# Running the last group's chains beside the next graph convolution's first four fifths

## The chip, the cores and the metric

The kernel runs on one core of one Trainium2 chip. The metric is device time in microseconds of one execution. Before the change three runs took 2504.49, 2504.52 and 2510.24 us; their median is 2504.52 us. A core has several engines that work beside each other, each through its own queue of instructions in order: TensorE (PE in the profile; PEld is its weight load), VectorE (DVE), ScalarE (ACT), GpSimd (POOL), and SyncE (SP), which here only issues transfers. They are tied to each other by semaphores.

## The reference

3125 nodes have 256 features each; 100,000 edges connect them. Four blocks follow each other, each of the form x = x + f(layernorm(x)):

1. a two-layer graph attention (four heads, then one);
2. a mixture of experts in which one choice holds for all tokens: the mean row picks two of eight experts, and every node goes through both;
3. a linear layer and two graph convolutions;
4. a routed mixture of experts, two of eight for each node.

The change lies where block 2 hands over to block 3, and where the two convolutions of block 3 meet. What is computed there:

```python
# block 2, after the choice of two experts with weights w_dense
h = gelu(xf @ W1[e] + b1[e]);  y = h @ W2[e] + b2[e]
out = layer_norm(sum_e w_dense[e] * y[e] + xf, gamma, beta)
# block 3
x = relu(input @ weight + bias)
for i in range(2):
    h = x @ conv_w[i]
    x = relu(segment_sum(h[src] * dinv[src] * dinv[dst], dst) + conv_b[i])
```

The segment sum over edges is a product with the matrix of edge counts, which an earlier stage has left in HBM as float16.

## The kernel before, in words

Nodes are padded to 25 blocks of 128 rows (`NB`, `P`); five blocks make a group (`GB`), and there are five groups (`GR`). `self.x` (`x_rows` in the profile) holds all rows. The program is written in an order of its own, but a framework that allots tiles also orders each engine's instructions by its own estimate of when each could start; so the order in which the queues are filled can differ from that of the source. Tiles come from stacked pools: a tile that takes the place of an earlier one has to wait until the earlier one's last readers are done. Where a tile lies thus decides what its first writer waits for.

**Second attention layer** (`graph_attention_fast`, `attend_all`). For each group and each of 25 source blocks DVE makes an exponent's argument `z` (L837), ACT the exponential (L839), DVE the weights `w` by a product with the counts (L845), and PE multiplies them with the rows (L854). There are two tiles for `z` and two for `w`. When a group ends, small tasks for it are taken from a queue `spare`, two at each step: sums to `x_rows` (L1009), then the tasks of `SharedExperts.tasks`: statistics (L1211, L1212), the root (L1216), normed rows into `xa` (L1220), transposes into `xa_t` (L1226, L1227) and their sum (L1231).

**Shared experts** (`SharedExperts.run`). `choose` computes the mean, the routing weights and the two experts' numbers with many small DVE operations on 8 columns (L1253 to L1286), loads the two experts' weights through SP (L1292, L1295), scales the second ones (L1316) and sums the second biases (L1329). POOL then adds the summed bias to `xa` (L1349) and `beta` to `x_rows` (L1350), 25 blocks each; ACT issues the loads of `gamma` and `beta` (L1342, L1344). After that, 256 rows at a time, PE makes the hidden product (L1377), ACT the Gelu (L1380), PE the second product (L1387), DVE the sum (L1390). Between these, `go_on` takes tasks from a queue of this function: for each group that is complete `finish(g)` (norm, L1024 to L1030, times gamma, L1367, added to `x_rows`, L1368), and the tasks that `before(g, tmp)` of the convolutions returns, here called a group's chain: `norm`, five transposes with copies (L1037, L1131), four blocks of the linear layer (L1137, L1140), and for each of five blocks `linear` (L1070), which projects the rows with the convolution's weights, scales them (L1073), cuts them in two parts whose sum is the number (L1075) and writes both to `parts[0]` (L1077 on ACT, L1078 on DVE). When the last block is done, all tasks that are left run, the last group's chain among them, and the room is given back.

**Convolutions** (`graph_convolutions_fast`, `layer`). For each group of five target blocks, five times: SP loads a block of counts (`cnt_h`, three tiles, L1090), ACT converts three fifths of it to the matmul's type (L1093) and DVE two fifths (L1094) into `cnt_r` (two tiles), and PE multiplies, five target blocks by five source blocks, 25 matmuls (L1099). During the first four of the five steps tasks of the queue `spare` are spread over the matmuls. After the fifth step `finish0` or `finish1` is called for each target block: DVE turns the sums into rows `o` (`total`, L1112, L1114), and in the first convolution two tasks are put in the queue, `turn` (transposes, L1037, Relu, L1161) and `linear(1, b, ...)`, the second convolution's projection. After the first convolution's last group a loop `while spare` runs what is left; then `router.open` allots its tiles and issues small loads (L2429 to L2454), and the second convolution starts. Its `finish1` adds to `x_rows` (L1173) and queues the router's tasks.

Of the kernel before, what the change touches and what calls it, by code (L numbers as in the profile page):

```python
# [11 lines left out]
F32 = mybir.dt.float32  # L12
F32R = mybir.dt.float32r
# [748 lines left out]
class Fast(Kernel):  # L762
# [277 lines left out]
    def graph_convolutions_fast(self, I, router, experts, out):  # L1040
# [5 lines left out]
        with ExitStack() as ctx:  # L1046
# [34 lines left out]
            spare = router.spare  # L1081

            def layer(i, work, finish):
                n = GB
                for b0 in range(0, NB, n):
                    pos = {}
                    for j0 in range(0, NB, 5):
                        ch = work.tile([P, 5, GW], F16, name="cnt_h", bufs=3)
                        o = b0 % GB * P
                        nc.sync.dma_start(ch[:, :, :n * P],  # L1090
                                          self.cnt[b0 // GB, :, j0:j0 + 5, o:o + n * P])
                        c = work.tile([P, 5, GW], F32R, name="cnt_r", bufs=2)
                        nc.scalar.copy(c[:, :3, :n * P], ch[:, :3, :n * P])  # L1093
                        nc.vector.tensor_copy(c[:, 3:, :n * P], ch[:, 3:, :n * P])  # L1094
                        for b in range(n):
                            if j0 == 0:
                                pos[b] = psum.tile([P, 512], F32, name="po")
                            for j in range(j0, j0 + 5):
                                nc.tensor.matmul(pos[b], lhsT=c[:, j - j0, ts(b, P)],  # L1099
                                                 rhs=parts[i][:, j].rearrange("p a m -> p (a m)"),  # L1100
                                                 start=(j == 0), stop=(j == NB - 1))
                            if j0 == NB - 5:
                                finish(b0 + b, pos[b])
                                continue
                            left = (NB - 5 - j0) // 5 * n - b
                            for _ in range(-(-len(spare) // left)):
                                spare.popleft()()

            def total(i, b, po, work):
                d = dinv[:, b:b + 1]  # L1110
                o = work.tile([P, D], F32, name="o", bufs=7)
                nc.vector.scalar_tensor_tensor(o, po[:, :D], d, conv_b[:, i, :], op0=ALU.mult,  # L1112
                                               op1=ALU.add)
                nc.vector.scalar_tensor_tensor(o, po[:, D:], d, o, op0=ALU.mult, op1=ALU.add)  # L1114
                return o

            with tc.tile_pool(name="gcn_first", bufs=1, reuse_waits="tile") as first:
                parts[0] = first.tile([P, NB, 2, D], F32R, name="parts0")

                def before(g, tmp):  # L1120
# [21 lines left out]
                    return ([norm] + [lambda b=b: turn(b) for b in range(GB)] +  # L1142
# [4 lines left out]
                with tc.tile_pool(name="gcn_in", bufs=1, reuse_waits="tile") as tmp:  # L1147
                    experts.run(lambda g: before(g, tmp))
                second = ctx.enter_context(ExitStack())
                room = second.enter_context(tc.tile_pool(name="gcn_second", bufs=1, side="right", reuse_waits="tile"))  # L1150
                parts[1] = room.tile([P, NB, 2, D], F32R, name="parts1")
                psum = second.enter_context(tc.tile_pool(name="gcn_po", bufs=5, space=PSUM, reuse_waits="tile"))
                with tc.tile_pool(name="gcn_work0", bufs=1, reuse_waits="tile") as work:
                    def finish0(b, po):
                        o = total(0, b, po, work)
                        turned = []

                        def turn():
                            x_t = work.tile([P, 2, P], F32, name="x_t", bufs=3)
                            turned.append(x_t)  # L1160
                            nc.scalar.activation(x_t, self.turn_block(aux, o), AF.Relu)  # L1161
                        spare.append(turn)
                        spare.append(lambda: linear(1, b, turned[0]))
                    layer(0, work, finish0)
                    while spare:
                        spare.popleft()()
# [4 lines left out]
            def finish1(b, po):  # L1171
                o = total(1, b, po, work)
# [11 lines left out]
class SharedExperts:  # L1184
# [8 lines left out]
    def open(self):  # L1193
        self.rooms = ExitStack()
        pool = self.rooms.enter_context(self.tc.tile_pool(name="ffn0", bufs=1, side="right", reuse_waits="tile"))

        self.xa = pool.tile([P, NB, D], F32, name="xa")
# [133 lines left out]
    def run(self, onward):  # L1331
# [3 lines left out]
        with ExitStack() as ctx:  # L1335
            pool = ctx.enter_context(tc.tile_pool(name="ffn0_w", bufs=1, reuse_waits="tile"))
# [4 lines left out]
            gamma = pool.tile([P, D], F32, name="gamma")  # L1341
            nc.scalar.dma_start(gamma, bcast(I["L0_ffn_gamma"], D))  # L1342
# [19 lines left out]
            def finish(g):  # L1362
                xa = self.xa[:, g * GB:(g + 1) * GB, :]
                k.norm_group(xa, xa, GB, work)
# [5 lines left out]
            for c0 in range(0, NP, n):  # L1370
# [13 lines left out]
                for b in range(c0 // P, c1 // P):  # L1384
# [5 lines left out]
                    nc.vector.tensor_add(self.xa[:, b, :], self.xa[:, b, :], py)  # L1390
                    if b % GB == GB - 1:
# [3 lines left out]
                    go_on(1)  # L1395
            while spare:
                spare.popleft()()
        self.rooms.close()
# [1492 lines left out]
```

## Time and profile before

| What | Value |
|---|---|
| median of three timed runs | 2504.52 us |
| profiled execution, own time | 2363.22 us |
| profiled execution, span | 2361.4 us |
| mean granted PE clock | 0.943 |
| PE, PEld, DVE, ACT, POOL busy | 2052.3, 1712.3, 1335.9, 1084.5, 807.8 us |
| second attention layer | about 1010 to 1294 us of the span |
| choice of experts, until the first expert matmul | 1294 to 1326 us |
| shared experts, with the chains | 1326 to 1567 us |
| first convolution | 1572 to 1739 us |
| second convolution | 1752 to 1935 us |
| routed experts | to the end, 2361 us |

The span is the time from the first to the last instruction of one execution that was taken with the profiler. That execution took 2363.22 us, 141 us less than the median of the timed runs, so its durations give the shape of the work, and sums made from them are compared with it first. A row of the timeline gives the start, the length, the engine, the line, the output and inputs, and in brackets how long the engine had been idle before and what ended that; rows that run into each other are merged, with their number behind an x. "SPq" and "ACTq" are those engines' queues as they issue transfers.

### The profile page before, as it was taken

The page shows a single profiled execution, that of the slowest core. Times are in us where ns is not written, and L with a number is a line of the kernel's source. Part 1 is how long each engine was busy: PE and PEld are TensorE (multiplying, and loading weights), DVE is VectorE, ACT ScalarE, POOL GpSimd, SP SyncE. Part 2 cuts the span into 40 slices and gives each one's busy share as a digit, 9 for nine tenths or more (in the row PEclk, how much of TensorE's full clock was granted, in tenths as well). Part 3 has the DMA queues.
Part 4 walks back from the last instruction along what each step waited for, and adds up shares of the span by engine and source line. Part 5 has one row for each costly group of instructions (what it writes and reads, how often), then busy time and mean ns, then how long its engine had stood idle before and what let it go on. Part 6 is the DMA issues. An engine that isn't in the chain of part 4 may idle for free. (4 is left out here: it accounts for less than half of the span.)

```text
span 2361.4 us, 35957 instructions
## 1 busy us (share of the span) xinstructions
PE 2052.3 (87%) x10512; PEld 1712.3 (73%) x10512; DVE 1335.9 (57%) x4399; ACT 1084.5 (46%) x2496; POOL 807.8 (34%) x801
## 2 busy tenths in 40 slices
PE   5577888878988876999999699979989978999996
PEld 5456677666766655778888588858877767888886
DVE  7898576767777763178888443333326664212221
ACT  3497556555666536044454254434434433222231
POOL 1777777777777723000000500000001223222221
PEclk9899899999999888989999799989999988999998
DMA  7545574756677758962221100023325445667773
GB/s 234 159 122 152 140 209 135 210 165 190 201 196 210 204 154 314 323 220 70 80 74 41 45 1 1 1 99 125 126 99 170 144 136 187 190 189 229 214 214 73
DMA packets 236521, 356.91 MB, mean 151 GB/s; under 512 B 37356, under 2 KB 177923, under 8 KB 232603
## 3 DMA queue, kind: packets, MB, share of 16 engines
q1 hardware_dynamic: 194315, 258.97, 33.8%
q0 software_dynamic: 39008, 92.91, 15.2%
q10 hardware_dynamic: 2992, 2.62, 0.4%
q8 instruction: 88, 1.44, 0.2%
q14 instruction: 118, 0.97, 0.1%
HBM read 268.69 MB, written 86.20 MB: 150 GB/s over the span
## 5 line engine op out<-in xcount | busy, mean ns | idle before, releaser
L1876 POOL DMA_INDIRECT edge_rows<-table,pick x566 | 590.8, 1044 | 183.5 <-issue 78.3
L1961 PE MATMUL edge_sums<-edge_moves,edge_rows 128*128 128x120 f32 x2264 | 332.3, 294 | 76.4 <-DVE agg L1974 75.9
L1961 PEld LDWEIGHTS edge_sums<-edge_moves,edge_rows 128*128 128x128 f32 x2264 | 308.5, 206 | 114.9 <-DVE agg L1974 93.4
L1099 PE MATMUL po<-parts,cnt_r 128*128 128x512 f32 x1250 | 310.1, 403 | 14.0 <-ACT cnt_r L1093 9.3
L1099 PEld LDWEIGHTS po<-parts,cnt_r 128*128 128x128 f32 x1250 | 236.1, 192 | 63.5 <-ACT cnt_r L1093 10.1
L854 PE MATMUL po<-h,w 128*128 128x257 f32 x1250 | 277.2, 383 | 3.5 <-ACT o L1006 2.3
L854 PEld LDWEIGHTS po<-h,w 128*128 128x128 f32 x1250 | 237.8, 192 | 38.5 <-ACT o L1006 3.9
L1764 PE MATMUL ps<-hot_key,hot_lo 128*128 128x350 f16 (+2 forms) x782 | 192.4, 335 | 67.4 <-DVE acc L1790 29.6
L1782 ACT CAST acc<-ps 128x325 f32 (+2 forms) x391 | 178.7, 457 | 134.4 <-PE ps L1764 98.6
L1744 DVE TENSOR_SCALAR hot_key<-iota_key,key 128x350 f16<-128x350 f16 (+2 forms) x782 | 235.9, 329 | 4.2 <-PE ps L1764 3.4
L2759 ACT ACTIVATE hid<-ph,ffn_b 128x256 f32<-128x256 f32 (+1 forms) x232 | 105.6, 455 | 263.1 <-PE ph L2757 260.6
L2757 PE MATMUL ph<-xe,ffn_w 128*128 128x256 f32 (+1 forms) x928 | 194.1, 367 | 3.3 <-DMA ffn_w<-in_L_ffn_W 3.3
L2772 POOL DMA_INDIRECT out<-y,to x53 | 82.6, 1558 | 315.9 <-DVE y L2771 173.3
L2767 PE MATMUL py<-ffn_w,hid 128*128 128x256 f32 x848 | 189.9, 381 | 0.9 <-ACT hid L2759 0.9
L2757 PEld LDWEIGHTS ph<-xe,ffn_w 128*128 128x128 f32 x928 | 165.2, 194 | 26.2 <-DVE rt_xt L1030 3.7
L2767 PEld LDWEIGHTS py<-ffn_w,hid 128*128 128x128 f32 x848 | 159.6, 191 | 21.3 <-ACT hid L2759 1.3
L839 ACT ACTIVATE z<-z,att_cols 128x640 f32<-128x640 f32 x125 | 103.0, 828 | 146.4 <-DVE z L837 120.1
L1750 ACT ACTIVATE hot_lo<-iota_key,lo 128x128 f16<-128x128 f16 x494 | 170.0, 395 | 0.0
L1764 PEld LDWEIGHTS <-hot_lo 128*128 128x128 f16 x782 | 72.8, 104 | 113.2 <-ACT hot_lo L1757 43.1
L1093 ACT CAST cnt_r<-cnt_h 128x1920 fp32r<-128x1920 f16 x50 | 89.9, 1799 | 110.8 <-PE po L1099 101.7
L2433 POOL IOTA earlier<- 128x128 f32 x1 | 0.2, 242 | 395.0 <-PE po L1099 395.0
L845 DVE TENSOR_TENSOR w<-z,cnt 128x640 f32<-128x640 f32 x125 | 102.4, 820 | 41.4 <-PE po L854 38.5
(422 smaller groups left out, 3249.5 us busy)
## 6 DMA issues: line engine op xcount, KB each, us to landing
ffn_w<-in_L_ffn_W SPq DMA_DIRECT2D x58, 1024.0 KB
cnt_h<-cnt SPq DMA_DIRECT2D x50, 800.0 KB
rows<-blank SPq DMA_DIRECT2D x109, 258.0 KB
cnt<-acc SPq DMA_DIRECT2D x50, 400.0 KB
cnt<-cnt SPq DMA_DIRECT2D x25, 800.0 KB
normed<-first_out SPq DMA_DIRECT2D x20, 640.0 KB
first_out<-first SPq DMA_DIRECT2D x56, 192.0 KB
edge_rows<-table,pick POOLq DMA_INDIRECT x566
```

Source lines behind the costliest of these rows:

```text
L839: nc.scalar.activation(z, z, AF.Exp, bias=cols[:, 0, j:j + 1], scale=-1.0)
L854: nc.tensor.matmul(pos[i][:, :D + 1], lhsT=w[:, ts(i, P)], rhs=moving[:, j, :D + 1], start=(j == 0), stop=(j == NB - 1))
L1099: nc.tensor.matmul(pos[b], lhsT=c[:, j - j0, ts(b, P)], rhs=parts[i][:, j].rearrange("p a m -> p (a m)"), start=(j == 0), stop=(j == NB - 1))
L1744: nc.vector.tensor_scalar(h[:, u, :NB * w], self.wide[:, :NB * w], self.key[:, t:t + 1], None, op0=ALU.is_equal)
L1750: nc.scalar.activation(l[:, u, :], self.wide[:, :P], AF.Abs, bias=self.lo[:, t:t + 1], scale=-1.0)
L1764: last = self.nc.tensor.matmul(ps[:, :n], lhsT=l[:, u, :], rhs=h[:, u, :n], start=(u == 0), stop=(u == CT - 1))
L1782: ins = self.nc.scalar.copy(self.acc[g][:, :, ds(o + 1, width(c) - 1)], self.parts[c][:, :, 1:])
L1876: return self.nc.gpsimd.indirect_dma_start(out=self.ring[:, e % (RB * BT), :], out_offset=None, in_=self.table, in_offset=bass.IndirectOff ...
L1961: nc.tensor.matmul(ps[:, f * 4 * w:f * 4 * w + EW], lhsT=self.rows_of(m)[:, e, ts(f, P)], rhs=self.spread[m % 3][:, e * 5 * w:e * 5 * w + EW],
L2757: nc.tensor.matmul(ph, lhsT=w1[:, c, ts(f, P)], rhs=xe[:, c, :], start=(c == 0), stop=(c == 1))
L2759: nc.scalar.activation(hid[:, f, :], ph, AF.Gelu, bias=b1[:, f:f + 1])
L2767: nc.tensor.matmul(py, lhsT=hid[:, f, ts(i, P)], rhs=w2[:, f, :], start=(f == 0), stop=(f == NF - 1))
```

## The change

`SharedExperts.run` no longer runs the last group's tasks itself. At the last block it first runs what the queue still holds (the chain of the group before), then appends `finish` and the chain of the last group, and returns the queue; `graph_convolutions_fast` adds it to `spare`, so `layer` hands it out. Four empty tasks stand in that chain as pauses. To let tiles live long enough, `gamma` and the norm's small tiles come from the pool `gcn_in` (`keep`), which stays open together with `gcn_first` and `gcn_work0` until the first convolution is over; `xa` keeps its room until the first `finish0`, which closes it and takes the room of `parts[1]`; `xa_t` is given back at the end of `run`. The loop `while spare` after the first convolution is gone, so its last group's tasks go to the second convolution; for that `o` and `x_t` come from an outer pool, `gcn_sums`. The tiles for `cnt_h` are two instead of three.

```diff
+            sums = ctx.enter_context(tc.tile_pool(name="gcn_sums", bufs=1, reuse_waits="tile"))
...
-                        ch = work.tile([P, 5, GW], F16, name="cnt_h", bufs=3)
+                        ch = work.tile([P, 5, GW], F16, name="cnt_h", bufs=2)
...
-            def total(i, b, po, work):
+            def total(i, b, po):
                 d = dinv[:, b:b + 1]
-                o = work.tile([P, D], F32, name="o", bufs=7)
+                o = sums.tile([P, D], F32, name="o", bufs=7)
...
-            with tc.tile_pool(name="gcn_first", bufs=1, reuse_waits="tile") as first:
+            room_of = lambda stack, name: stack.enter_context(
+                tc.tile_pool(name=name, bufs=1, reuse_waits="tile"))
+            with ExitStack() as first_rooms:
+                first = room_of(first_rooms, "gcn_first")
                 parts[0] = first.tile([P, NB, 2, D], F32R, name="parts0")
...
-                    return ([norm] + [lambda b=b: turn(b) for b in range(GB)] +
+                    wait = [lambda: None] * 2 if g == GR - 1 else []
+                    return (wait + [norm] + wait + [lambda b=b: turn(b) for b in range(GB)] +
...
-                with tc.tile_pool(name="gcn_in", bufs=1, reuse_waits="tile") as tmp:
-                    experts.run(lambda g: before(g, tmp))
+                tmp = room_of(first_rooms, "gcn_in")
+                spare.extend(experts.run(lambda g: before(g, tmp), tmp))
                 second = ctx.enter_context(ExitStack())
-                room = second.enter_context(tc.tile_pool(name="gcn_second", bufs=1, side="right", reuse_waits="tile"))
-                parts[1] = room.tile([P, NB, 2, D], F32R, name="parts1")
...
+                def finish0(b, po):
+                    if parts[1] is None:
+                        experts.rooms.close()
+                        parts[1] = second.enter_context(tc.tile_pool(
+                            name="gcn_second", bufs=1, side="right", reuse_waits="tile")).tile(
+                                [P, NB, 2, D], F32R, name="parts1")
+                    o = total(0, b, po)
...
-                    layer(0, work, finish0)
-                    while spare:
-                        spare.popleft()()
+                layer(0, room_of(first_rooms, "gcn_work0"), finish0)
...
-    def run(self, onward):
+    def run(self, onward, keep):
...
+            gamma = keep.tile([P, D], F32, name="gamma")
+            nc.scalar.dma_start(gamma, bcast(I["L0_ffn_gamma"], D))
             pool = ctx.enter_context(tc.tile_pool(name="ffn0_w", bufs=1, reuse_waits="tile"))
...
-            gamma = pool.tile([P, D], F32, name="gamma")
-            nc.scalar.dma_start(gamma, bcast(I["L0_ffn_gamma"], D))
             beta = pool.tile([P, D], F32, name="beta")
...
-                k.norm_group(xa, xa, GB, work)
+                k.norm_group(xa, xa, GB, keep)
...
+                    if b == NB - 1:
+                        go_on(len(spare))
                     if b % GB == GB - 1:
                         g = b // GB
                         spare.append(lambda g=g: finish(g))
                         spare.extend(onward(g))
-                    go_on(1)
-            while spare:
-                spare.popleft()()
-        self.rooms.close()
+                    if b < NB - 1:
+                        go_on(1)
+        self.turned.close()
+        return spare
```

More of the change, by code (lines that the diff above doesn't have):

```diff
@@ L1145, in before, with turn @@
                              for b in range(GB)])
-                with tc.tile_pool(name="gcn_in", bufs=1, reuse_waits="tile") as tmp:
-                    experts.run(lambda g: before(g, tmp))
+                tmp = room_of(first_rooms, "gcn_in")
+                spare.extend(experts.run(lambda g: before(g, tmp), tmp))
                 second = ctx.enter_context(ExitStack())
-                room = second.enter_context(tc.tile_pool(name="gcn_second", bufs=1, side="right", reuse_waits="tile"))
-                parts[1] = room.tile([P, NB, 2, D], F32R, name="parts1")
                 psum = second.enter_context(tc.tile_pool(name="gcn_po", bufs=5, space=PSUM, reuse_waits="tile"))
[L1153 to L1163, printed above, removed]
-                    layer(0, work, finish0)
-                    while spare:
-                        spare.popleft()()
+                def finish0(b, po):
[5 more added lines that the diff above has]
+                    o = total(0, b, po)
+                    turned = []
+                    def turn():
+                        x_t = sums.tile([P, 2, P], F32, name="x_t", bufs=3)
+                        turned.append(x_t)
+                        nc.scalar.activation(x_t, self.turn_block(aux, o), AF.Relu)
+                    spare.append(turn)
+                    spare.append(lambda: linear(1, b, turned[0]))
+                layer(0, room_of(first_rooms, "gcn_work0"), finish0)
             router.open(ctx, aux, I)
@@ L1171, in finish1 @@
             def finish1(b, po):
-                o = total(1, b, po, work)
+                o = total(1, b, po)
                 nc.vector.scalar_tensor_tensor(self.x[:, b, :], o, 0.0, self.x[:, b, :],
@@ L1193, in open @@
     def open(self):
-        self.rooms = ExitStack()
-        pool = self.rooms.enter_context(self.tc.tile_pool(name="ffn0", bufs=1, side="right", reuse_waits="tile"))
-        self.xa = pool.tile([P, NB, D], F32, name="xa")
+        self.rooms, self.turned = ExitStack(), ExitStack()
+        room = lambda stack, name: stack.enter_context(
+            self.tc.tile_pool(name=name, bufs=1, side="right", reuse_waits="tile"))
+        self.xa = room(self.rooms, "ffn0").tile([P, NB, D], F32, name="xa")
+        pool = room(self.turned, "ffn0_turned")
         self.xa_t = pool.tile([P, 2, NP], F32, name="xa_t")
```

## The prediction

> **What bounds the kernel now.** I read the page first. TensorE is busy for 2052.3 of 2361.4 us (87%), so time is won where it idles or runs at a lower clock. The table of stages finds these places (columns: stretch, its length, busy time of PE, PE's weight load, DVE, ACT and POOL, granted PE clock, DMA share, GB/s):
>
> ```profile
> core 0: us, PE busy (x) PEld busy (x) DVE busy (x) ACT busy (x) POOL busy (x), PEclk, DMA share, GB/s
> 1294.00:1326.00 32.00, 6.21 (x22) 3.64 (x21) 24.02 (x86) 7.37 (x17) 17.20 (x26) 0.58 0.28 86
> 1544.00:1572.00 28.00, 13.66 (x47) 9.20 (x47) 13.14 (x42) 11.08 (x24) 0.00 (x0) 0.70 0.19 69
> 1572.00:1603.00 31.00, 31.00 (x129) 25.52 (x130) 8.69 (x15) 9.64 (x6) 0.00 (x0) 0.94 0.50 176
> 1738.00:1752.00 14.00, 7.85 (x36) 5.38 (x34) 7.61 (x25) 7.63 (x17) 1.55 (x8) 1.00 0.49 180
> ```
>
> Three thin stages: the choice of experts (1294), the end of the shared experts (1544, the change's first place) and the seam between the convolutions (1738, its second). Next the timeline of the first seam (start, length, engine, line):
>
> ```profile
> 1543.16 0.40 ACT L1077 CAST parts<-split 128x256 fp32r<-128x256 f32 x1 [0.20 <-DVE split L1075]
> ...
> 1565.85 123.32 SPq L1090 DMA_DIRECT2D cnt_h<-cnt  x22
> 1570.12 3.70 ACT L1093 CAST cnt_r<-cnt_h 128x1920 fp32r<-128x1920 f16 x2 [3.02 <-DMA cnt_h<-cnt]
> 1571.97 31.45 PE L1099 MATMUL po<-parts,cnt_r 128*128 128x512 f32 x130 [6.20 <-ACT cnt_r L1093]
> 1579.69 1.80 ACT L1093 CAST cnt_r<-cnt_h 128x1920 fp32r<-128x1920 f16 x1 [5.86 <-PE po L1099]
> 1585.36 1.80 ACT L1093 CAST cnt_r<-cnt_h 128x1920 fp32r<-128x1920 f16 x1 [3.86 <-PE po L1099]
> ```
>
> The first count block is loaded only at 1565.85, lands 4.2 us later, is converted in 1.8 us, and the convolution starts at 1571.97. Conversions follow PE's release: 5.67 us for 25 matmuls, but 7.72 for the first 25, at a granted clock of 0.77. A cold start costs 2.05 us. Then the choice:
>
> ```profile
> 1304.89 17.05 POOL L1350 TENSOR_TENSOR x_rows<-x_rows,beta 128x256 f32<-128x256 f32 x25 [10.55 <-DMA beta<-in_L_ffn_beta]
> ...
> 1307.04 0.65 DVE L1264 TENSOR_SCALAR load<-rw 128x8 f32<-128x8 f32 x1
> ...
> 1319.85 1.21 SPq L1292 DMA_DIRECT2D ffn_w<-in_L_ffn_W  x2
> ```
>
> While POOL adds beta, DVE's little operations with two SBUF inputs or a tensor_scalar take 0.65 us; reciprocals, and the same forms where POOL rests, some 0.2. They lead to the expert numbers, these to the weight loads at 1319.85.
>
> **The change, part by part.** The order in which each engine's instructions are queued in the two built kernels decides what really moves.
>
> *First seam.* In the built order the five projections (L1070) of the group before last still precede the convolution on PE; the last group's chain stands between the 37th and the 100th of the first 125 count matmuls. The loads no longer wait for the chain's tiles: the first waits for PE's last reads of the expert weights (hidden product ended by 1534.6, second product 1538.9), so it lands by 1543.2. On ACT the first conversion stands behind the cast of 1543.16: 1543.56 + 1.80 = 1545.4, where PE can start. The group then is 125 x 0.2267 = 28.3 us, plus the chain's own PE work: 5 pairs of transposes at 0.27 (1.3), 4 weight blocks at 1.07 (4.3), 5 projections at 0.86 (4.3), 9.9 in all. In later groups, five pairs of transposes and projections already run between count matmuls: 34.2 us a group, 28.3 + 5.65 + 0.2 of stall, so such interleaving works. 1545.4 + 28.3 + 9.9 = 1583.6, against 1602.36 before: 18.8 less. I take off 1.3 for stalls: normed rows reach PE about 0.2 late (the first rows' conversion delays DVE by 0.83), ACT's conversions stand ahead of copies of transposes. **-17.5**, between -12 (half the chain's 14 steps wait 0.8 for ACT) and -19.
>
> Does the cover hold? DVE has 8.69 us busy and ACT 9.64 in the 31 us of that group before; the chain is most of the 13.14 and 11.08 of the 28 us ahead, and all of it has 38 us to fit into. Without cover the chain would again cost its 21 us (1545.4 to 1566.7) and the gain be the earlier load and conversion alone.
>
> *Second seam.* Here the built order does not do what the diff says: on PE all five transposes and projections of the last group still stand ahead of the second convolution's first count matmul. Only ACT's and DVE's first conversions move, ahead of the last block's split:
>
> ```profile
> 1747.80 0.41 ACT L1077 CAST parts<-split 128x256 fp32r<-128x256 f32 x1
> ...
> 1750.14 3.48 ACT L1093 CAST cnt_r<-cnt_h 128x1920 fp32r<-128x1920 f16 x2
> 1751.98 36.16 PE L1099 MATMUL po<-parts,cnt_r 128*128 128x512 f32 x151 [3.08 <-ACT cnt_r L1093]
> ```
>
> The block is loaded from 1741.27, so landed by 1745.5; converted from 1748.2 it is ready at 1750.0: -1.9. The pause of PE shrinks from 2.9 us (projections end 1749.1) to 1.0. The Trainium skill ("TensorE: Matmul & The Clock Gate", Part 1) puts half clock after about 3.4 us idle in a free-running window. The row disagrees in size: here 2.9 us were enough to lose it (7.68 us for the first 25 matmuls, clock 0.78). By the rule as written neither seam would start cold; by the row 1.0 us lies far under, and the 1.6 us of the first seam less clearly. I take warm starts: -2.0 more here, **-3.9** in all; between 0 and -4. (The first seam's warm start is in its sum; cold, it is 2.05 worse.)
>
> *Beta.* Gamma moves to the tiles that live on, and with it beta's place. This is no line of the change's plan: in the built order ACT issues beta's load before the second attention layer, not near its end, and POOL puts 20 of the 25 adds ahead of the iota that waits for that layer's end. They run group by group as the rows are normed (L1220). In the choice, 17 DVE operations take 11.2 us from start to start; free ones of 8 columns take 0.20 to 0.27: 17 x 0.22 = 3.7. Gain 7.4, less 0.4 for the last five adds beside the last norms: **-7.0** (-5 to -8.2), all on the path: the numbers release the weight loads, these L1316 and the first Gelu.
>
> *What the 20 adds cost where they go.* PE bounds attention (231.7 of 234 us), two weight tiles deep:
>
> ```profile
> 1081.24 1.38 DVE L1220 TENSOR_SCALAR xa<-x_rows,ln_mv,ln_rstd 128x256 f32<-128x256 f32 x4
> 1082.54 0.81 DVE L845 TENSOR_TENSOR w<-z,cnt 128x640 f32<-128x640 f32 x1
> 1084.39 0.81 DVE L845 TENSOR_TENSOR w<-z,cnt 128x640 f32<-128x640 f32 x1
> ```
>
> PE starts on the first of these tiles at 1083.71, the next at 1086.16: slack 0.4 and 1.0. The Trainium skill ("SBUF — State Buffer", Who interferes with whom) says that GpSimd and VectorE share a port pair, an exclusive lock for the whole instruction. That speaks against the change: by it each add blocks DVE for its 0.72, 20 x 0.72 = 14.4. The rows charge less: L904 runs every 0.87 us beside POOL's bias adds, 0.43 alone, and the choice's operations 0.67 instead of 0.22; 0.44 an add, 8.8 in all. Laying 0.44 an add from 1081.7 on, the first tile comes 0.5 late, the next 0.3 more: 0.8 a group, four groups, **+3.2** (0 to +9, or +14.4 less slack of 4 by the rule).
>
> *The rest.* The conversion buffers before the count tiles go from three to two. A load goes out when a conversion ends and is needed two steps later: 2 x 5.67 - 1.80 = 9.5 us against 4.2 to land; hidden by 5.3. In the second convolution SP's five stores of rows (5.5 us) pass one load, which is then needed some 4 us after landing. Zero. The sums and the turned tile live in an outer pool and the second convolution's parts take their place later: no instruction more. Zero.
>
> Sum: +3.2 - 7.0 - 17.5 - 3.9 = **-25.2**, from 2363.2 of the profiled execution (span 2361.4) to 2338.0. The timed runs have a median of 2504.5, 141 us more; no row says where. Idle time and few PE instructions are concerned, so I carry the difference over unscaled: 2479.3.
>
> **Rivals.** (1) *Attention pays in full.* The lock as in the rule: +10.4 instead of +3.2, 2486.5. For it: two tiles only. Against: the measured 0.44.
> (2) *The chain is not hidden.* PE, in order, waits for ACT behind the conversions at most of the 14 steps; the first seam gives only load, conversion and clock, 4.2 + 1.8 + 2.0 = 8: 2488.8. For it: one in-order ACT queue. Against: the later groups' 0.2 of stall.
> (3) *Slower: two buffers for counts.* If loads took over 9.5 us from issue to landing, each of some 48 steps would wait for the excess at L1093. At 9.5 + 0.53 the whole 25.2 is gone; at 10.3 it is 2504.5 + 13 = 2517. Against: 4.2 measured with two in the queue, and a DMA share of 0.45.
> (4) *No change.* Freed time returns as a later wait. Against: PE is over 90% busy in most later slices, so work just moves up. 2504.5.
>
> **How the numbers follow.** Forecast 0.70, rivals (1) and (2) 0.09 each, (3) 0.06, (4) 0.03, better than all bounds 0.03. The forecast's own range is 2471 (every gain at its top and attention free, -31.2, times 2504.5 / 2363.2) to 2488; the range 2471 to 2495 adds (1) and (2), with both at their ends, and holds some 0.85. Under 0.3% (7.5 us) a measurement of this kernel can't be told from no change; so faster 0.91, same 0.03, slower 0.06.
>
> **What would show it.** Right: first count matmul about 1.5 us after the last projection, its group some 39 us long and ending about 18 earlier; the L1264-like operations at 0.2; first seam's and second seam's first 25 matmuls at 5.7. Wrong: PE waits for L845 above 10 us in attention; gaps before the interleaved chain's matmuls; ACT waiting for the count loads inside the convolutions; or a cold clock at both starts, 4 us worse.

## The result, and the profile after

The changed kernel takes 2496.42 us in the median of nine runs (2490.97 to 2505.14), the kernel before 2510.24 in the median of nine (2504.49 to 2515.72). The ratio is 0.9948 (95% interval 0.9931 to 0.9964): 13 us less, between 9 and 17. The forecast was 25.2 less; about half of it came.

The profiled execution of the changed kernel has a span of 2496.0 us, that of the kernel before 2361.4. This is no gain or loss of the change: before the second attention layer starts, the one needs 1161.6 us and the other 1010.8, and the kernel before, profiled again on other chips, needs 1157.2 and 1148.9. On one chip, used for the last two runs below, the kernel before took 2365.5 us and on all others 2505 to 2512. So the forecast's 141 us without a row lie in the edge stage and most likely belong to the chip, and the comparison is made stage by stage. The table gives stretches between marks that both traces have (first and last instruction of a line), of the kernel before in three profiles (the first, e1 and e12).

| Stretch | before, three profiles | after | change, from the second | foretold |
|---|---|---|---|---|
| first layer's last normalised rows (L941) to attention's first matmul (L854) | 70.6, 70.3, 70.7 | 76.6 | +6.4 | 0 |
| attention, first to last matmul | 283.3, 283.3, 283.4 | 289.9 | +6.6 | +3.2 |
| from there to the first Gelu (L1380, L1388 after) | 37.3, 37.3, 36.5 | 29.7 | -7.6 | -7.0 |
| first Gelu to the end of the last second product | 207.6, 207.6, 207.6 | 207.6 | 0 | 0 |
| from there to the end of the first convolution's group 1 | 63.3, 63.3, 63.0 | 45.9 | -17.4 | -17.5 |
| its groups 2 to 5 | 136.8, 136.8, 136.8 | 138.8 | +2.0 | 0 |
| seam between the convolutions | 12.9, 12.9, 12.9 | 10.9 | -2.0 | -1.9 |
| second convolution's group 1 | 30.3, 30.3, 31.2 | 28.7 | -1.6 | -2.0 |
| its groups 2 to 5 | 147.4, 147.4, 149.7 | 149.5 | +2.1 (0 from the third) | 0 |
| from there to the end | 431.7, 431.9, 433.1 | 433.5 | +1.6 (+0.4 from the third) | 0 |

Without the last two rows, which move as much between two executions of one kernel, the sum is 6.4 + 6.6 - 7.6 - 17.4 + 2.0 - 2.0 - 1.6 = -13.6, and the timed runs say -13. Two rows held what was not foreseen and one was mis-sized.

Groups are counted in the table and in this text within each convolution, from 1; the recorded expectations count all ten from 0, so that their groups 1 to 4 are the first convolution's 2 to 5, and their 7 and 8 the second one's third and fourth. First the stages that the forecast showed, in the table of stages of the changed kernel (the choice until the first expert matmul, the first seam, the group after it, the second seam):

```profile
core 0: us, PE busy (x) PEld busy (x) DVE busy (x) ACT busy (x) POOL busy (x), PEclk, DMA share, GB/s
1451.50:1476.00 24.50, 7.18 (x23) 4.44 (x24) 16.45 (x86) 7.44 (x17) 4.71 (x8) 0.55 0.40 116
1689.00:1695.00 6.00, 3.44 (x15) 2.32 (x13) 4.80 (x15) 5.15 (x9) 0.00 (x0) 1.00 0.42 138
1695.00:1734.60 39.60, 39.50 (x172) 31.29 (x173) 18.85 (x53) 18.06 (x29) 0.00 (x0) 1.00 0.37 125
1873.40:1884.30 10.90, 6.77 (x31) 4.54 (x29) 5.21 (x20) 6.79 (x15) 1.55 (x8) 1.00 0.45 156
```

The same 86 DVE operations of the choice now take 16.5 us instead of 24.0. The first seam has shrunk to 6 us, and the group after it takes 39.6 us in which PE is recorded as busy for 39.5: the chain's work fills it. Its start in the timeline:

```profile
1692.94 0.41 ACT L1077 CAST parts<-split 128x256 fp32r<-128x256 f32 x1 [0.20 <-DVE split L1075]
...
1693.25 1.79 ACT L1094 CAST cnt_r<-cnt_h 128x1920 fp32r<-128x1920 f16 x1
...
1695.09 8.89 PE L1100 MATMUL po<-parts,cnt_r 128*128 128x512 f32 x37 [1.54 <-ACT cnt_r L1094]
```

The load no longer ends the wait, the first conversion does, right behind the cast; PE pauses 1.54 us instead of 6.2. In the choice, timeline of the same kernel:

```profile
1456.20 3.72 POOL L1358 TENSOR_TENSOR x_rows<-x_rows,beta 128x256 f32<-128x256 f32 x5 [4.50 <-DVE xa L1227]
...
1464.19 0.17 DVE L1271 TENSOR_SCALAR load<-rw 128x8 f32<-128x8 f32 x1
...
1469.57 1.20 SPq L1299 DMA_DIRECT2D ffn_w<-in_L_ffn_W  x2
```

Five additions are left here, and the little operation that took 0.65 us takes 0.17. The other twenty run in the attention layer, where the forecast had two tiles a group to be late by 0.8 together. One such group in the timeline (the idle time of PE stands in the brackets of its row):

```profile
1232.31 2.21 DVE L1227 TENSOR_SCALAR xa<-x_rows,ln_mv,ln_rstd 128x256 f32<-128x256 f32 x4
...
1232.81 3.56 POOL L1358 TENSOR_TENSOR x_rows<-x_rows,beta 128x256 f32<-128x256 f32 x4 [78.98 <-DVE xa L1227]
1234.44 1.34 DVE L845 TENSOR_TENSOR w<-z,cnt 128x640 f32<-128x640 f32 x1
1235.71 0.81 DVE L1227 TENSOR_SCALAR xa<-x_rows,ln_mv,ln_rstd 128x256 f32<-128x256 f32 x1
...
1235.84 2.43 PE L854 MATMUL po<-h,w 128*128 128x257 f32 x10 [1.08 <-DVE w L845]
...
1236.60 1.30 POOL L1358 TENSOR_TENSOR x_rows<-x_rows,beta 128x256 f32<-128x256 f32 x1 [0.23 <-DVE xa L1227]
1237.23 1.35 DVE L845 TENSOR_TENSOR w<-z,cnt 128x640 f32<-128x640 f32 x1
```

Before, the four normalisations took 1.38 and the product 0.81 (rows in the forecast), and the fifth normalisation 0.40:

```profile
1083.27 0.40 DVE L1220 TENSOR_SCALAR xa<-x_rows,ln_mv,ln_rstd 128x256 f32<-128x256 f32 x1
```

Now the four and the product take 2.21 and 1.34, 1.36 more, with four additions beside them that take 0.89 each instead of 0.68. The fifth normalisation takes 0.41 more, and the next product, beside the fifth addition, 0.54 more. PE waits 1.08 for the first tile and a little for the second: the 50 matmuls around it take 13.5 us instead of 12.0. Groups 2 to 5 of the attention are longer by 1.5, 1.5, 1.5 and 1.8 us, the first by 0.3; that is the 6.6 of this row.

### The profile page after: what moved, and what is told of

Same layout as the page of the kernel before. It is cut to its first block, busy times and chain, and to the rows that moved or that the text cites. A ratio compares the mean times of both kernels' runs of the same rounds, so it can differ in the third digit from the quotient of the medians.

```text
span 2496.0 us, 35950 instructions
## 1 busy us (share of the span) xinstructions
PE 2107.8 (84%) x10512; PEld 1739.7 (70%) x10512; DVE 1349.4 (54%) x4399; ACT 1086.5 (44%) x2496; POOL 809.0 (32%) x801
## 5 line engine op out<-in xcount | busy, mean ns | idle before, releaser
L1971 PE MATMUL edge_sums<-edge_moves,edge_rows 128*128 128x120 f32 x2264 | 352.2, 305 | 82.1 <-issue 59.1
L1971 PEld LDWEIGHTS edge_sums<-edge_moves,edge_rows 128*128 128x128 f32 x2264 | 327.9, 217 | 124.6 <-issue 73.8
L1100 PE MATMUL po<-parts,cnt_r 128*128 128x512 f32 x1250 | 315.7, 405 | 7.7 <-DVE ng_st L1024 2.7
L1774 PE MATMUL ps<-hot_key,hot_lo 128*128 128x350 f16 (+2 forms) x782 | 204.9, 355 | 126.8 <-ACT hot_lo L1767 29.0
L854 PE MATMUL po<-h,w 128*128 128x257 f32 x1250 | 278.9, 384 | 8.1 <-DVE w L845 5.8
L854 PEld LDWEIGHTS po<-h,w 128*128 128x128 f32 x1250 | 237.4, 191 | 45.2 <-DVE w L845 7.8
L1754 DVE TENSOR_SCALAR hot_key<-iota_key,key 128x350 f16<-128x350 f16 (+2 forms) x782 | 238.1, 334 | 33.8 <-PE ps L1774 12.9
L1984 DVE TENSOR_TENSOR agg<-agg,edge_sums 128x126 f32 (+1 forms) x283 | 87.4, 309 | 183.8 <-remote 64.5
```

The source lines that it names most:

```text
L854: nc.tensor.matmul(pos[i][:, :D + 1], lhsT=w[:, ts(i, P)], rhs=moving[:, j, :D + 1], start=(j == 0), stop=(j == NB - 1))
L1100: nc.tensor.matmul(pos[b], lhsT=c[:, j - j0, ts(b, P)], rhs=parts[i][:, j].rearrange("p a m -> p (a m)"), start=(j == 0), stop=(j == NB - 1))
L1754: nc.vector.tensor_scalar(h[:, u, :NB * w], self.wide[:, :NB * w], self.key[:, t:t + 1], None, op0=ALU.is_equal)
L1774: last = self.nc.tensor.matmul(ps[:, :n], lhsT=l[:, u, :], rhs=h[:, u, :n], start=(u == 0), stop=(u == CT - 1))
L1971: nc.tensor.matmul(ps[:, f * 4 * w:f * 4 * w + EW], lhsT=self.rows_of(m)[:, e, ts(f, P)], rhs=self.spread[m % 3][:, e * 5 * w:e * 5 * w + EW],
```

## The experiments

All numbers of stretches are from the trace of the kernel named. A kernel without a ratio was run once.

**The kernel before, twice more (e1, e12).**

> The kernel before, profiled once more, because its first profiled execution was 141 us shorter than its timed runs. If those 141 us lie in the stages ahead of the second attention layer (the theory), the stages from there on repeat to about 1 us each: attention 283.3, from its end to the first Gelu 37.3, Gelu to the end of the second product 207.6, from there to the first count matmul 33.0, first convolution 167.1, seam 12.9, second convolution 177.7, routed part 431.7 us. If the first profile was unusual in these stages too (rival), attention or the routed part comes out some us longer, and the comparison by stages has to be made anew.

Measured: 283.3, 37.3, 207.6, 33.0, 167.1, 12.9, 177.7, 431.9, as in the first profile to 0.2 us. The stages from attention on can be compared; the difference lies in the edge stage ahead of it. A third time:

> The kernel before, profiled a third time. In both its profiles groups 7 and 8 of the convolutions took 36.2 and 45.7 us (81.9 together); in all kernels with any edit, two of which only moved tiles of the first convolution by 32 bytes, 83.3 to 90.2. Theory (the length of these groups varies by execution, with the scatters of the router's rows): 83 or more here too in this execution or a value between. Rival (something of the unedited program itself): 81.9 a third time.

Measured: 36.9 and 47.2 for groups 7 and 8, 84.1 together. So these two vary by execution, and the +2.1 of the table's last but one row need not be the change's.

**Early beta alone (e2).**

```diff
-            spare = router.spare
+            spare = router.spare; sums = ctx.enter_context(tc.tile_pool(name="gcn_sums", bufs=1, reuse_waits="tile"))
...
-                o = work.tile([P, D], F32, name="o", bufs=7)
+                o = sums.tile([P, D], F32, name="o", bufs=7)
...
-                            x_t = work.tile([P, 2, P], F32, name="x_t", bufs=3)
+                            x_t = sums.tile([P, 2, P], F32, name="x_t", bufs=3)
...
-                        ch = work.tile([P, 5, GW], F16, name="cnt_h", bufs=3)
+                        ch = work.tile([P, 5, GW], F16, name="cnt_h", bufs=2)
```

> One part of the change alone: the outer pool for the sums and two count buffers in the kernel before. That brings beta's load and 20 of the 25 additions into the second attention layer; the seams keep their order. Theory (the additions cost attention 1.5 us in each of four groups, as the changed kernel's trace has it): attention 283.3 + 6.5 = 289.8, attention's end to the first Gelu 37.3 - 7.6 = 29.7, all else as before: -1 us in all, 2509 where the kernel before has 2510. Rival (the longer attention comes from something else in the change): attention stays at 283.3 and the time falls by 7 to 8. For two count buffers: no wait of ACT for the loads, groups of the first convolution 34.36 us as before (theory), or over 34.8 (rival: the 0.5 us that each of these groups lost in the changed kernel comes from the buffers).

Measured: attention 289.8, choice 28.9, groups 34.36: as the theory has it. POOL's first additions in this kernel, in attention though `gamma` stays in its old pool:

```profile
1231.48 3.55 POOL L1350 TENSOR_TENSOR x_rows<-x_rows,beta 128x256 f32<-128x256 f32 x4 [79.20 <-DVE xa L1220]
```

Two things more came with it. The second seam is 10.9 and the group after it 28.7, the whole gain of the changed kernel there, without a task deferred. (e2 brings the pool and the two buffers together. In programs built with the pool alone and with the buffers alone, which were not run, only the pool puts ACT's first conversion ahead of the last block's split; and e5, with three buffers in the second convolution, keeps the seam at 10.9.) And the time is 1.0014 of the kernel before (0.9997 to 1.0030), not 3 to 6 us less, as its stretches from attention on add up to: something ahead of attention had got longer (see e13).

**Additions behind the choice (e3).**

```diff
-            beta = pool.tile([P, D], F32, name="beta")
-            nc.scalar.dma_start(beta, bcast(I["L0_ffn_beta"], D))
...
-                nc.gpsimd.tensor_add(k.x[:, b, :], k.x[:, b, :], beta)
             work = ctx.enter_context(tc.tile_pool(name="ffn0_work", bufs=2, reuse_waits="tile"))
+            beta = work.tile([P, D], F32, name="beta", bufs=1)
+            nc.sync.dma_start(beta, bcast(I["L0_ffn_beta"], D))
+            for b in range(NB): nc.gpsimd.tensor_add(k.x[:, b, :], k.x[:, b, :], beta)
```

> The changed kernel with the 25 additions of beta moved behind POOL's additions of the bias, beside the experts' matmuls (beta in a tile whose place comes free after the choice, loaded by SP). Theory (the additions slow DVE where it feeds PE, and nowhere else): attention back from 289.9 to 283.3, the choice stays at 29.7, experts 207.6 as before: 6 to 7 us less than the changed kernel, about 2490 where that has 2496. Rival (the additions cost as much beside the experts, where DVE normalises): experts longer by 3 to 8 us and no gain.

Measured: attention 283.8, choice 29.9, experts 207.6; 2493.09 us, ratio 0.9932 (0.9912 to 0.9952). POOL's rows in its timeline: the 25 additions now follow those of the bias, beside the experts.

```profile
1437.75 0.15 POOL L2408 IOTA part<- 128x1 f32 x1 [291.61 <-PE po L854]
1460.95 18.03 POOL L1355 TENSOR_TENSOR xa<-xa,ffn_b_sum 128x256 f32<-128x256 f32 x25 [23.05 <-ACT ffn_b_sum L1336]
1478.95 17.14 POOL L1359 TENSOR_TENSOR x_rows<-x_rows,beta 128x256 f32<-128x256 f32 x25
```

By the stages it is shown that the additions cost attention its 6 us and that they cost nothing beside the experts. The ratio is 4 us better than the changed kernel's, but the two intervals overlap.

**Where the count tiles lie (e4, e6, e7, e9, e10).** Groups 2 to 5 of the first convolution lost 0.49 us each; where nothing else runs, their count matmuls start every 233.3 ns instead of 226.7 (the recorded texts have 233.5 and 227). The two buffers and the outer pool were cleared by e2, whose groups keep 34.36. What is left is that the pool `gcn_in` now stays open below the count tiles and moves them, so I moved them alone. In the changed kernel:

```diff
+                room0 = room_of(first_rooms, "gcn_work0"); room0.tile([P, 8], F32, name="pad")
...
-                layer(0, room_of(first_rooms, "gcn_work0"), finish0)
+                layer(0, room0, finish0)
```

with 8, 24 and 56 columns (32, 96 and 224 bytes) for e4, e6 and e9; in the kernel before the same 32 bytes ahead of its count tiles (e7), or ahead of `parts0`, which moves both (e10).

> The changed kernel with 32 bytes left free ahead of the count tiles of the first convolution, so that cnt_r starts at 32 bytes past a multiple of 64 again, as it does in the kernel before and in the second convolution of both. Nothing else differs. Theory (the place of the tile sets the cadence of the count matmuls, 233.5 ns instead of 227): groups 1 to 4 of the first convolution back from 34.85 to 34.37 us, the first from 39.5 to about 39.0; 2 to 2.5 us less in all, about 2494 where the changed kernel has 2496. Rival (two buffers, or the clock): 34.85 stays, no gain.

> The changed kernel with 96 bytes left free ahead of the count tiles of the first convolution, so that cnt_h and cnt_r start 96 bytes past a multiple of 128, as in every convolution profiled so far whose matmuls kept 227 ns; 0 and 32 bytes past it went with 233.5 ns. Theory (the place within 128 bytes counts): blocks 4 and 5 of groups 1 to 4 at 227 ns, these groups 34.37 us, 2 us less in the first convolution. Rival (something else in the changed kernel): 233.5 ns and 34.86 us again.

> The kernel before with 32 bytes left free ahead of the count tiles of the first convolution: cnt_r at a multiple of 128 there, nothing else changed. Theory (the place within 128 bytes counts): blocks 4 and 5 of its groups at 233.5 ns, groups 1 to 4 34.86 us instead of 34.37, 2.5 us longer in the first convolution. Rival: 227 ns and 34.37 us stay.

> The changed kernel with 224 bytes left free ahead of the first convolution's count tiles: cnt_r then lies 224 bytes past a multiple of 256, like parts0 in every kernel so far and like cnt_r wherever the matmuls kept 227 ns; 0, 32 went with 233.5 and 96 with 232 ns. Theory (the place within 256 bytes counts): blocks 4 and 5 of groups 1 to 4 at 227 ns, these groups 34.37 us, the first convolution 2 to 2.5 us shorter than in the changed kernel (176). Rival (the place has a longer period, or the cause is another): 232 ns or more.

> The kernel before with 32 bytes left free ahead of parts0, so that parts0 and cnt_r of the first convolution both start at a multiple of 256 instead of 224 past it. Theory one (what counts is where the two operands lie relative to each other): 227 ns and 34.37 us, as in the kernel before. Theory two (what counts is the place of cnt_r by itself): 233.5 ns and 34.86 us, as when cnt_r alone was moved.

| Kernel | parts0, bytes past a multiple of 256 | cnt_r, the same | group of five steps, us | matmul, median ns |
|---|---|---|---|---|
| before (e1) | 224 | 224 | 34.36 | 389 |
| after | 224 | 0 | 34.86 | 396 |
| e4 | 224 | 32 | 34.86 | 396 |
| e6 | 224 | 96 | 34.78 | 393 |
| e9 | 224 | 224 | 34.37 | 389 |
| e7 | 224 | 0 | 34.86 | 395 |
| e10 | 0 | 0 | 34.37 | 389 |

The rows for the last fifty count matmuls of group 3, in the changed kernel,

```profile
L1100 PE MATMUL po<-parts,cnt_r x49: 395/396/396, 1792.4 to 1803.6; 128*128 128x512 f32 x49
```

and with the 224 bytes (e9), smallest, median and largest duration in ns:

```profile
L1100 PE MATMUL po<-parts,cnt_r x50: 389/389/389, 1793.0 to 1804.1; 128*128 128x512 f32 x50
```

My first theory (64 bytes) and the second (128) fell. The matmuls are quick where the tile of the stationary operand (`cnt_r`) and that of the moving one (`parts0`) lie at the same place within 256 bytes, be it 224 or 0, and in none of the other three placements tried. That is a rule from seven kernels and five placements, for one shape. The misplaced tile costs the changed kernel some 2 us in the first convolution. The gain of e9 in the timed runs (ratio 0.9945, 0.9925 to 0.9966) can't be told from the changed kernel's; e4 has 0.9943 (0.9927 to 0.9958).

**Three count buffers in the second convolution (e5).** `bufs=2` became `bufs=2 + i`.

> The changed kernel with three count buffers in the second convolution and two in the first as it has them. Theory (two buffers cost the second convolution something after all: in all four kernels with two, the first scatter of the router's rows keeps DVE 4.7 to 4.9 us instead of 3.5, and groups 7 and 8 take 1.3 to 8.6 us more together than with three): group 7 back to 36.15 and group 8 to 45.7, the second convolution 176.1 us instead of 178.2; 2 us less than the changed kernel on average, more where its group 7 is as long as 42 us. Rival (the longer groups come from the tiles' other places, or by chance): 36.9 and 47 again.

Measured: groups 7 and 8 36.5 and 47.2, ratio 0.9949 (0.9930 to 0.9969): the rival. Two buffers cost nothing that shows here, as forecast. In e4, group 7 even took 42.0; its timeline shows DVE held for 4.71 us by a copy that waits for the router's scatter, with the rows behind it, for which PE's next group waits:

```profile
1951.06 0.17 DVE L2562 COPY rt_row<-rt_mark 128x2 f32<-128x2 f32 x1 [4.71 <-DMA rows<-rt_row,rt_index]
```

**The chain written ahead of the convolution (e8).**

```diff
-                spare.extend(experts.run(lambda g: before(g, tmp), tmp))
+                for task in experts.run(lambda g: before(g, tmp), tmp): task()
```

> The changed kernel with the last group's chain written ahead of the first convolution again instead of handed out among its matmuls; the tiles' places stay, so the loads still come early, and in the built order all of the chain stands on PE between the 21st and the 29th count matmul. Theory (the spreading over the matmuls is what hides the chain's waits): the first count matmul still 1.5 us after the last projection, but PE then waits for the norm, about 3.5 us, and for the five to seven hand-overs to ACT inside the chain, some 6 us: the first group about 49 us instead of 39.5, 8 to 10 us more than the changed kernel (2505), still some 5 less than the kernel before. Rival (the early load alone brings the gain, the order is free): first group 39.5 to 41.

Measured: the first group takes 42.35 us instead of 39.53, 1.6 of it a start at half clock; the ratio is 0.9948 (0.9928 to 0.9969), like the changed kernel's. PE waits once, 1.0 us, and then runs the chain as a block:

```profile
1694.69 5.24 PE L1100 MATMUL po<-parts,cnt_r 128*128 128x512 f32 x15 [1.53 <-ACT cnt_r L1094]
1700.92 1.66 PE L1100 MATMUL po<-parts,cnt_r 128*128 128x512 f32 x6 [1.00 <-DVE cnt_r L1095]
1702.42 0.38 PE L1037 MATMUL aux<-ident,xa 128*128 128x128 f32 x2
...
1704.70 2.35 PE L1141 MATMUL aux<-xn_t,gcn_w 128*128 128x320 f32 x8
1706.64 1.10 PE L1100 MATMUL po<-parts,cnt_r 128*128 128x512 f32 x3
1707.66 2.42 PE L1141 MATMUL aux<-xn_t,gcn_w 128*128 128x320 f32 x8
1709.92 4.72 PE L1070 MATMUL aux<-gcn_w,x_t 128*128 128x256 f32 x20
```

My expectation was far off, the rival's near. The early loads are what pays here; the framework itself puts 21 count matmuls ahead of the chain once the tiles allow it, and the norm is done when they are. Handing the chain out is worth some 1 us.

**A faster version (e11).** The edits of e3 and e9, and in the first convolution each block's transposes queued one step ahead of the projection of the block before:

```diff
-                    spare.append(turn)
+                    spare.insert(max(len(spare) - 1, 0) if b % GB else len(spare), turn)
```

> The changed kernel with three edits: the additions of beta behind the choice, the 224 bytes, and in the first convolution each block's transposes queued one step ahead of the projection of the block before. Theory: attention 283.5 instead of 289.9 (-6.4), first convolution -2.3, and at the second seam PE no longer waits for ACT between a block's transposes and its projection (five waits of 0.6): the seam 8.5 us instead of 10.9; together -11, about 2485 where the changed kernel has 2496. Rival (ACT's order still holds the first conversion, so the seam stays): -8.5, 2488.

Measured: 2489.78 us, ratio 0.9916 (0.9897 to 0.9935), some 21 less than the kernel before. Attention takes 283.9, groups 2 to 5 34.19 each, but the seam 11.1: the rival was right there. PE is done 3.3 us before it can go on, because ACT's first conversion stands behind the last block's cast, and after this pause the second convolution starts at half clock:

```profile
1876.32 0.41 ACT L1077 CAST parts<-split 128x256 fp32r<-128x256 f32 x1 [0.36 <-DVE split L1075]
...
1876.63 3.48 ACT L1094 CAST cnt_r<-cnt_h 128x1920 fp32r<-128x1920 f16 x2
...
1878.47 2.07 PE L1100 MATMUL po<-parts,cnt_r 128*128 128x512 f32 x4 [3.30 <-ACT cnt_r L1094]
```

**What the first iota waits for (e13, e14).** By the stretches from attention on, the changed kernel should be 20 us faster, and it was 13. In all nine profiles of the kernels so far that have the outer pool, attention began 75.7 to 77.2 us after the last normalised rows, in the five without it 70.3 to 70.7. POOL's timeline there, of the kernel before (e1):

```profile
1092.24 0.15 POOL L1250 IOTA expert<- 128x8 f32 x1 [27.27 <-issue]
1092.34 0.23 POOL L438 IOTA rk_before<- 128x64 f32 x1
1145.95 0.72 POOL L787 PARTITION_ALL_REDUCE ends_all<-ends  x1 [53.37 <-DVE ends L785]
```

and of the changed kernel, with two rows of DVE:

```profile
1142.69 0.15 POOL L1257 IOTA expert<- 128x8 f32 x1 [80.16 <-PE po L947]
1142.79 0.23 POOL L438 IOTA rk_before<- 128x64 f32 x1
1143.78 0.15 DVE L785 TENSOR_SCALAR ends<-ends 128x1 f32<-128x1 f32 x1
1153.46 0.37 POOL L787 PARTITION_ALL_REDUCE ends_all<-ends  x1 [10.43 <-issue]
1153.94 0.22 DVE L799 TENSOR_SCALAR att_cols<-sd,ends_all 128x25 f32<-128x25 f32 x1
```

The outer pool lies below the pools of the choice and shifts them by 10,240 bytes. So `expert`, which the first iota fills, moves from a place where rows had been read early to one that holds the weights PE reads until the last matmul of L947. The iota waits some 50 us longer, and behind it, in order, stands what the all-reduce needs. The queue's rows of L787 in the changed kernel:

```profile
L787 POOLq MODIFY_POOL_CONFIG  x2: 11/11/11, 1143.2 to 1143.3; - x2
L787 POOL PARTITION_ALL_REDUCE ends_all<-ends x1: 373/373/373, 1153.5 to 1153.5; - x1
```

From this configuration to the all-reduce pass 10.2 us in which nothing is recorded, although its input `ends` is written by 1143.9. Before (e1), the configuration came at 1092.8, 53 us ahead of need, and the all-reduce followed 0.3 us after `ends`. All DVE columns for attention (L799) wait for the all-reduce. That the 10.2 us are the loading of code is not shown by a row. The Trainium skill ("GPSIMD Engine Reference", 2.1 Instruction dispatch) would explain them: the first call to freshly loaded code pays about 6 us for it without a visible instruction, measured there from the configuration on; here the gap is longer. In e13 the two tiles stand at the front of their pool, over the early rows again:

```diff
-        before = pool.tile([P, 8, 8], F32, name=name + "_before")
+        before = pool.tile([P, 8, 8], F32, name=name + "_before") if getattr(self, "rk", None) is None else self.rk
...
-        wr = route.tile([P, 2, 8], F32, name="wr")
+        expert, k.rk = route.tile([P, 8], F32, name="expert"), route.tile([P, 8, 8], F32, name="rk_before"); wr = route.tile([P, 2, 8], F32, name="wr")
...
-        expert = route.tile([P, 8], F32, name="expert")
...
-        k.ranks(rank, rw, route, "rk0", 1)
+        k.ranks(rank, rw, route, "rk0", 1); k.rk = None
```

> The changed kernel with the two small tiles that POOL's iotas of the choice fill, expert and the ranks' comparison, moved to the front of their pool: there they lie again over rows that are read early (as in the kernel before), not over the weights that PE reads until the first layer's end. Nothing is taken out. Theory (in the changed kernel the first iota waits 50 us longer for PE's L947, POOL's next 10.4 us of issue then stand between the last h and the all-reduce L787, and attention starts 6 us later after the first layer's norm): from the end of the rows' normalising (L941) to the first attention matmul 70.6 us instead of 76.4, as in the kernel before; all later stages as in the changed kernel: 6 less than its 2496, 2490. Rival (the 6 us between L941 and attention come from elsewhere): 76.4 stays, no gain.

> The same with the three edits of the faster kernel before it (additions of beta behind the choice, 224 bytes, transposes one step ahead). Theory: 70.6 us to attention, attention 283.5, and from attention's start to the end 1325 as there: 6 less than its 2490, 2484, 27 below the kernel before. Rival: 2490.

These two ran on the chip on which the kernel before takes 2365.53 us. e13: 2348.13, ratio 0.9921 (0.9904 to 0.9937), 19 us less; e14: 2341.12, ratio 0.9891 (0.9875 to 0.9908), 26 less. Attention begins 70.6 and 70.5 us after the rows, POOL's row in e13:

```profile
942.31 0.15 POOL L1257 IOTA expert<- 128x8 f32 x1 [27.89 <-issue]
...
996.02 0.37 POOL L787 PARTITION_ALL_REDUCE ends_all<-ends  x1 [53.38 <-DMA check_row<-ends_row]
```

The 6 us are found, by taking their cause away: the stage shows it, while the intervals of e13's ratio and the changed kernel's still overlap. e14 has the lowest ratio of all.

## Where the prediction was right, and which steps failed

The mechanisms of all three gains held. What failed are two terms of cost: the zero for "the rest", that is for tiles in other places, and the size of what the additions cost attention.

- *First seam, -17.5.* Right, -17.4, and by its own steps: the load out of the way, the conversion behind the cast (1693.25, start at 1695.09), the group about 39 us. That it fits to 0.1 is partly luck. The 1.3 us that I took off for stalls were used up, but PE has no recorded wait in that group; its count matmuls start every 233 ns or so instead of the sum's 226.7, and later than that behind a piece of the chain. That the chain would be covered was right. That it has to be handed out for this was not: e8 gets nearly the same without.
- *Second seam, -3.9.* Right in size (-2.0 and -1.6) and in that PE's order did not move. It is the pool of the sums that gives it (e2), the deferred tasks nothing. The pause before was 3.08 us, as its row says, where I wrote 2.9, and a start at half clock cost 1.6 us against the same group started warm, where I had 2.05. That the start turns warm held in eight of the nine profiles with the pause of 1.05 us.
- *Beta, -7.0.* Right in size, -7.6 (7.0 to 8.6 among the kernels without these twenty additions in the choice). The reason given for it, that `beta` moves with `gamma`, did not hold: in e2 `gamma` stays, and the additions come early all the same. The outer pool is enough.
- *What the 20 adds cost where they go, +3.2.* Wrong in size: +6.6 (5.4 to 6.9 among the kernels that have it). The mechanism and the price are right: DVE's rows are longer by 1.36 + 0.41 + 0.54 = 2.31 us a group, 0.46 an addition, where I had 0.44; the full lock, as the forecast priced it, would be 0.72. The step that failed is "the first tile comes 0.5 late, the next 0.3 more". I laid the additions over DVE's old durations; but both engines stretch each other, so four additions fell on the first tile and not two. Of the 2.31 us PE pays 1.5 in each of three groups and 1.8 in the last, and not 0.8.
- *The rest, zero.* Wrong, twice. "The sums and the turned tile live in an outer pool ... no instruction more. Zero." The outer pool moved every tile above it. That cost 6.0 to 6.4 us through POOL's first iota (e13). The pool `gcn_in`, which stays open and for which the forecast has no term, moved the count tiles, and their place cost some 2 us (e9). I had asked what the moved tiles' own loads wait for, and for `beta` had found that it comes earlier; I had not asked it of the tiles that the diff doesn't name. The zero for two count buffers held.

With these three, 6.4 + 2.0 + (6.6 - 3.2) = 11.8, the forecast of -25.2 becomes -13.4, and -13 was measured. The upper end that I gave the forecast itself, 2488, was also too low for its own terms: with each at its worst (-12, 0, -5, +9) they sum to -8, that is 2496.5. No rival was right alone: attention paid some 6.6 of the 10.4 of rival (1), the chain was hidden (2), the buffers cost nothing (3), and what came back of the freed time was not a later wait but the three items above (4).

## What to carry to other kernels

A pool put below others moved every tile above it here: compare the places of all tiles and what their first writers now wait for, also in stages that the change doesn't touch, and on each in-order queue ask what stands behind the first writer. A step laid beside another engine's work is paid by what it covers once both are stretched, not by the old durations. When stages add up to more than the clock gives, the rest lies in a stage that was not compared.

## What the hardware showed beyond that

- The place of the two operands of a matmul relative to each other within 256 bytes made 3% of its rate (a start every 226.7 or 233.3 ns; 232.4 at a distance of 128 bytes). The Trainium skill ("SBUF — State Buffer", Who interferes with whom) gives PE two independent read ports, one for the moving operand and one for the weight load, and says nothing of their places; from that I would expect no effect, and the measurement decides. Why there is one is open.
- A pause of PE of 3.08 to 6.26 us stood ahead of thirteen profiled starts of a convolution; in all thirteen the granted clock was 0.5 at the first matmul or from at most 1.03 us after it. With a pause of 1.05 to 1.54 us this happened in 5 of 19 starts, from at most 0.51 us after the first matmul: at the first seam in e3, e8, e9 and e14, at the second in e5. Each of these five cost 1.5 to 1.6 us. A stretch of half clock lasted 3.4 or 6.8 us in the records. That fits the free-running window of 3.4 us that the forecast weighed, but not that a pause must fill it. PE was also thinly used ahead of the pause (busy 3.44 of 6.0 us in the changed kernel's first seam); which of these decides is open.
- One chip ran the kernel before in 2365 us and others in 2505 to 2512. In the three profiles of the faster kind (the first, e13 and e14) the difference of some 140 to 150 us lies in the stage of the edges, ahead of everything changed here; why is open.
